# Turning two x1n tiles by VectorE and DRAM in place of TensorE in a retention and FFN kernel

## The chip, the cores and the metric

The kernel runs on one core of a Trainium2 chip. The metric is the device time of one execution in microseconds; the lower the better. A core has five engines that run their own instruction streams in order: TensorE (PE; its weight loads are a row of their own, PEld), VectorE (DVE), ScalarE (ACT), GpSimd (POOL) and SyncE (SP), which here issues nearly all DMAs.

## The reference

4096 tokens (4 sequences of 1024) of width 512 go through a retention layer and an FFN, each with a layer norm in front and behind:

```python
def attn(x):                       # x normalised
    q, v = x @ Wq.T, x @ Wv.T
    ret = scan(v)                  # state = lam * state + v_t, by head
    out = layernorm(q * ret) * gamma + beta
    return (out * silu(x @ Wg.T)) @ Wo.T

def ffn(x):                        # x normalised, weights rounded to fp8 and back
    gate = silu((x @ gate_w) * gate_scale)
    return ((gate * ((x @ up_w) * up_scale)) @ down_w) * down_scale

x1  = x  + layernorm(attn(layernorm(x)))
out = x1 + layernorm(ffn(layernorm(x1)))
```

Everything is float32. The inner width of the FFN is 1536.

## The kernel before

The tokens are cut into eight blocks of 512 (NB = 8), each of four tiles of 128 tokens. The main loop (lines 1048 to 1328) has one turn t for each block and in it twelve steps i, one for each 128 columns of the FFN's inner width. In step i of turn t TensorE does the gate, up and down matmuls of block t's FFN (`f`, an object of `Ffn`; down lags two steps behind), and between them pieces of the retention of block t + 1 (`b`) and, late in the turn, of block t + 2 (`n`). `l` is the FFN of the block before, whose end is done in the first steps. The order of all instructions on every engine is the order in which the code writes them (`InOrder`, line 66): a wait on an engine holds everything behind it on that engine.

**Retention of a block from 2 on ("fast").** Each of the four projections v, q, g, o is done as seven products on halves (a scheme after Strassen and Winograd), so a block has 28 products. `order` (line 333) is the list of them by projection and number j, and `product` (line 481) does the next one: 8 matmuls, then the work on the result (a copy, an addition into `mids`, for some j a scan or a gate), and it also issues the DMA that fetches the weights of the product four places on into a ring of four (`fetch_weights`, line 384). Right operands with sums in them are made on GpSimd by `input_sums` (line 465), which writes t_sums 0 to 3 from the turned input xnT: sums 1 and 2 serve products 5 and 6, sums 3 and 4 products 7 and 4. For v the order of j is 1, 2, 6, 7, 4, 5, 3. Product 2 of v ends in two scans on VectorE.

**From o to x1n.** When po of a tile is complete, `o_moments` takes its mean and variance on VectorE (bn_stats and bn_aggr) and the power -1/2 on GpSimd; `x1_of` normalises it on ScalarE (`shift_scale`), adds it to x on GpSimd and stores x1 to DRAM (`kept`); `x1_moments` does the statistics of x1; `x1n_of` normalises x1 on VectorE (`center_scale`). Then x1n has to be turned, so that the width lies along the partitions: the FFN's matmuls read it as x1nT, in two parts, an upper one (`upper_of`, a cast on ScalarE) and the rest (`rest_of`, a subtraction on VectorE).

In turns 1 to 5 the four tiles are turned in two ways. Tiles 0 and 1 go through `move_x1n` and `turn_by_blocks` (line 311): VectorE transposes blocks of 32 x 32, four DMAs a tile write them to DRAM with the blocks in their new places, one DMA loads the tile. Tiles 2 and 3 are turned by TensorE in step 11 (`turn_x1n`, line 751: four transposes a tile into PSUM, tile pt). The next turn's first gate (line 1088) reads all four tiles of x1nT, the whole of both parts.

The input of the block after, xn, is turned in the same turns by `send_x` and `fetch_x` (lines 443 and 457): VectorE transposes blocks, one DMA a tile writes them to DRAM (mx), and after the fourth tile four DMAs fetch a quarter of the partitions each into xnT.

**Order in steps 9 to 11 of turns 1 to 5**, by engine where it matters:

- Step 9: gate; the last product of o; x1_moments of tiles 0 and 1; up; fuse (VectorE multiplies gate and up, ScalarE casts the product); x1n_of, block transpose and DRAM writes of tiles 0 and 1, then their two loads; input_sums 1 and 2 of n; o_moments of tiles 2 and 3; down.
- Step 10: gate; x1_of of tiles 2 and 3; up; fuse; x1_moments of tiles 2 and 3; x1n_of of tile 2; down.
- Step 11: gate; up; n's product v1; fuse; x1n_of of tile 3; the rest of fuse of step 10 (`f.rest(10)`, in the other steps at the step's start); input_sums 3 and 4; upper and rest of tiles 0 and 1; down; transposes, upper and rest of tiles 2 and 3; n's products v2 and v6.
- Step 0 of the next turn: rest of fuse of step 11; gate; product v7; up; fuse; product v4; down; product v5.

In turn 6 there is no n; tiles 2 and 3 are turned by TensorE there too. In turn 1 ScalarE also runs a search for values out of range over the weights (`find_over`), whose scratch lies in buffers that the transposes use.

Of the kernel before, what the change touches and what calls it, by code (L numbers as in the profile page):

```python
# [10 lines left out]
F32 = mybir.dt.float32  # L11
# [6 lines left out]
P = 128  # L18
# [5 lines left out]
def retention_ffn_sandwich(  # L24
# [20 lines left out]
    NT, D = x.shape  # L45
    I = gate_w.shape[1]
    NC = D // P
# [3 lines left out]
    NB = NT // TB  # L51
    Q = 32
    NQ = P // Q
# [5 lines left out]
    work = ctx.enter_context(tc.tile_pool(name="work", bufs=2))  # L59
    small = ctx.enter_context(tc.tile_pool(name="small", bufs=3))  # L60
    dram = ctx.enter_context(tc.tile_pool(name="dram", bufs=2 * NS, space=bass.MemoryType.DRAM))
# [249 lines left out]
    def turn_by_blocks(dst, src, tag, name):  # L311


        t = work.tile([P, NQ, NC, Q], F32, tag=tag, name=name)
        dve.transpose(t, src.rearrange("p (c a i) -> p a c i", c=NC, a=NQ))
        m = dram.tile([P, NQ, NC, Q], F32, tag="turn", name=f"m{name}", bufs=3)
        for b in range(NQ):
            sp.dma_start(
                m[:, b].rearrange("(a i) c j -> i a (c j)", a=NQ),
                t[ts(b, Q)].rearrange("i a c j -> i a (c j)"),  # L320
            )
        return lambda: sp.dma_start(dst, m)
# [7 lines left out]

    FAST = 2
    H = TB // 2
    order = [("v", j) for j in (1, 2, 6, 7, 4, 5, 3)]
    order += [("q", j) for j in (1, 6, 2, 7, 4, 5, 3)]
    order += [("g", j) for j in (1, 2, 6, 7, 4, 5, 3)]
    order += [("o", j) for j in (1, 2, 6, 5, 3, 7, 4)]
    banks = {
        "v": {1: 0, 6: 1, 5: 0}, "q": {1: 1, 6: 0, 5: 1},
        "g": {1: 0, 6: 0, 5: 1}, "o": {1: 0, 6: 1, 5: 0},
# [38 lines left out]
            sp.dma_start(operands[k][j], t)  # L378

    RING = 4  # L380
    total_products = len(order) * (NB - FAST)
    fetched = [0]

    def fetch_weights():
        n = fetched[0]
        if n < total_products:
            k, j = order[n % len(order)]
            sp.dma_start(w_ring[:, n % RING], operands[k][j])
            fetched[0] += 1

    class Retention:
# [88 lines left out]

        def product(self):

            k, j = order[self.made]
            n = (self.t - FAST) * len(order) + self.made
            self.made += 1
            w = w_ring[:, n % RING]
            if j in (1, 6, 5):
                bank = ps_tile(f"p{k}{j}_{self.t}", f"pa{banks[k][j]}").rearrange("p (c f) -> p c f", c=2)
                if j == 6:
                    self.bank_b = bank  # L490
                else:
                    self.bank_a = bank
            bank = self.bank_b if j in (6, 7, 4) else self.bank_a
            for o in range(2):
                out_ = bank[:, o]
                if k != "o" and len(self.right[j].shape) == 4:
                    out_ = out_.rearrange("p (g j) -> p g j", j=Q)
                for c in range(2):
                    if k == "o":
                        left, right = self.left[j][:, c, ts(o, P)], w[:, c, :]  # L500
                    else:
                        left, right = w[:, c, ts(o, P)], self.right[j][:, c]
                    pe.matmul(
                        out_, left, right,
                        start=(j in (1, 6, 5) and o == 0 and c == 0), stop=True,
                        skip_group_check=True,
                    )
            fetch_weights()
            if k == "o":
                return self.add_o(j, bank)  # L510
            c12, p1, s167 = (mids[:, m] for m in (1, 2, 3))
            if k == "v" and self.t == FAST:

                if j == 1:
                    self.p1 = work.tile([P, 2, H], F32, tag="rstd", name="p1", bufs=1)
                p1 = self.p1
            if j == 1:
                act.copy(p1, bank)
            elif j == 6:
                dve.tensor_tensor(c12, bank, p1, ALU.add)  # L520
            elif j == 7:
                dve.tensor_tensor(s167, bank, p1, ALU.add)
            elif j == 2:
                self.take(k, 0, 0, bank)
            elif j == 4:
                dve.tensor_tensor(p1, bank, p1, ALU.add)
                self.take(k, 1, 0, p1)
            elif j == 5:
                dve.tensor_tensor(s167, bank, s167, ALU.add)
                self.take(k, 1, 1, s167)  # L530
            else:
                dve.tensor_tensor(c12, bank, c12, ALU.add)
                self.take(k, 0, 1, c12)
# [195 lines left out]
        def x1_of(self, s):  # L729
            self.x1n[s] = work.tile([P, D], F32, tag="tok", name=f"x1n_{self.t}_{s}", bufs=4)  # L730
            center = shift_scale if self.fast else self.center
            center(self.x1n[s], self.po.pop(s), self.mvo[s])
            pool.tensor_tensor(self.xt[s], self.xt[s], self.x1n[s], ALU.add)
            self.kept[s] = dram.tile([P, D], F32, tag="kept", name=f"kept_{self.t}_{s}")
            sp.dma_start(self.kept[s], self.xt[s])

# [17 lines left out]
        def move_x1n(self, s):  # L754

            x1n = self.x1n.pop(s)
            dst = x1n.rearrange("p (b c j) -> p b c j", b=NQ, c=NC)
            self.pt[s] = dst.rearrange("p b c j -> p c b j")
            return turn_by_blocks(dst, x1n, "ret", f"xs1_{self.t}_{s}")

        def part(self, h, s):
            part = self.x1nT[:, h, :, ts(s, P)]
# [152 lines left out]
    a = Retention(0, x_first)  # L915
# [84 lines left out]
    a.o_moments(0)  # L1000
    rounds(1)
    a.x1_of(0)
    a.o(1, "pd1")
    a.o_moments(1)
    a.x1_moments(0)
    a.x1_of(1)
    a.x1n_of(0)
    a.o(2, "pd2")
    a.o_moments(2)
    a.x1_moments(1)  # L1010
    a.x1_of(2)
    a.x1n_of(1)
    a.o(3, "pd3")
    a.new_x1nT()
# [2 lines left out]
    a.o_moments(3)  # L1017
    a.x1_moments(2)
    a.x1_of(3)
    a.x1n_of(2)  # L1020
    a.rest_of(0)
    b.q(0, "pf")
# [25 lines left out]
    for t in range(NB):  # L1048
        f, n = Ffn(a), None
        fast = b is not None and b.fast  # L1050
        for i in range(NI):
            if t > 0 and (t > 1 or i) and not (fast and i == 11):
                (f if i else l).rest((i - 1) % NI)
            if t == 0 and i == 0:
                n = Retention(2)
# [36 lines left out]
            for _ in range(look[i][0] if t == 1 else 0):  # L1092
                next(search)

            if fast and i < 10:
                b.product()
            if t == 2 and i == 0:
                next(passing)
# [44 lines left out]
            if fast and i == 7:  # L1143
                b.y_sums(3, 4)
            if fast and i == 9:
                b.x1_moments(0)
                b.x1_moments(1)
            if fast and i == 10:
                b.x1_of(2)
                b.x1_of(3)  # L1150
            units()
            f.up(i)
            if n and i == 11:
# [3 lines left out]
            if t == 0 and i == 10:  # L1157
# [1 line left out]
                keep_sums("g")  # L1159
                load()  # L1160
                b.o_moments(3)
            if b and i == 11:
                b.x1n_of(3, center_scale)
            if fast and i == 11:
                f.rest(10)
            if n and i == 11:
                n.input_sums(*((3, 4) if fast else (1, 2)))
            if t == 0 and i == 11:
                b.upper_of(2)
            if fast and i == 9:  # L1170
                loads = []
                for s in range(2):
                    b.x1n_of(s)
                    loads.append(b.move_x1n(s))
                for load in loads:
                    load()
                if n:
                    n.input_sums(1, 2)
            if fast and i == 11:
                for s in range(2):  # L1180
                    b.upper_of(s)
# [33 lines left out]
            if fast and i == 8:  # L1215
# [1 line left out]
                b.o_moments(1)  # L1217
                b.x1_of(0)
                b.x1_of(1)
            if fast and i == 9:  # L1220
                b.o_moments(2)
                b.o_moments(3)
            if fast and i == 10:
                b.x1_moments(2)
                b.x1_moments(3)
                b.x1n_of(2)
            if t == 0:
                if i == 3:
                    rounds(2, now=False)
                    b.halves()  # L1230
                    units()
                    rounds(1, now=False)
                elif i < 8:
                    rounds(3, now=False)
                if i == 2:
                    b.halves()
                if i < 11:
                    f.rest(i)
                if i < 2:
                    n.stats(i)  # L1240
# [7 lines left out]
                n.new_xnT()  # L1248
            if b and not fast and 7 <= i <= 10:
                b.x1_of(i - 7)  # L1250
            if b and not fast and i >= 9:
                b.rest_of(i - 9)
            if n and t > 0 and i in (6, 7):
# [28 lines left out]
            if n and i == 11:  # L1282
                if t == 0:
                    n.product()
                else:
                    b.turn_x1n(2, "pf")
                    b.upper_of(2)
                    b.rest_of(2)
                b.turn_x1n(3, "pf")
                b.upper_of(3)  # L1290
                b.rest_of(3)
                if t == 0:
                    n.input_sums(3, 4, engine=dve)
                    f.rest(11)
            if fast and (i < 3 or i in (7, 8)):
                b.product()
            if fast and i == 2:
# [6 lines left out]
                b.var()  # L1304
                b.rstd_y()
            if n and i == 11:
                n.products(2 if t else 1)
            if n and t > 0 and i == 5:
                n.stats(0)
                n.stats(1)  # L1310
# [86 lines left out]
```

## Time and profile before

| | us |
|---|---|
| median of 3 runs | 972.82 |
| lowest, highest | 972.75, 974.45 |
| the profiled execution | 973.82 |
| its span, first to last instruction | 972.0 |

The page of the profiled execution gives for each engine the time in which it was busy and the share of the span; "PE 957.4 (98%)" is TensorE's. The granted clock of TensorE was 0.997 of full speed. A line of the timeline gives start, duration, engine, code line, operation, tiles (out<-in) and shape, how many instructions it merges, and in brackets the idle time of the engine in front of it with what ended it. All code lines are L74, the helper that records every operation, so the tiles' names tell what a line is: pfg is the gate's result, pfu up's, pd down's, pv a product of v, pt the transposed x1n, t_sums the input sums, mx the DRAM copy of xn, mxs that of tiles 0 and 1 of x1n, mv the statistics.

The costliest groups of instructions by TensorE are up (205.1 us), gate (198.1) and down (189.4), 768, 768 and 720 matmuls of 128x512 that follow each other about 0.23 us apart. The 68 transposes into pt, 8 of them in each of turns 1 to 5, are recorded with 275 ns each; they overlap.

### The profile page before, as it was taken

The numbers are of one execution on the slowest core, as the hardware profiler recorded it, in microseconds if no ns is written. First come the engines' busy times: TensorE is split into PE (matmuls) and PEld (weight loads), VectorE is DVE, ScalarE is ACT, GpSimd is POOL, SyncE is SP. The second block draws the span as 40 slices with busy tenths as digits, with TensorE's granted clock in tenths as the row PEclk, the third lists the DMA queues.
The fourth block names the chain that finished last, engine by engine and source line by source line (L and its number), as shares of the span: only waits on it lengthen the run. The fifth ranks groups of instructions, "written<-read, shape, count | busy, mean of one in ns | idle before, by whom it ended". The sixth has DMA issues, their size and how long they took to land.

```text
span 972.0 us, 11798 instructions
## 1 busy us (share of the span) xinstructions
PE 957.4 (98%) x4118; PEld 764.9 (79%) x4118; DVE 678.5 (70%) x1038; ACT 406.2 (42%) x637; POOL 283.1 (29%) x356
## 2 busy tenths in 40 slices
PE   9999999999999999999999999999999999999996
PEld 7455767678888888888888888888888888888885
DVE  5996999666767577586685766867667676757535
ACT  3555675458655135431433315332153421524223
POOL 1405121402327042250523405242142512314020
PEclk9999999999999999999999999999999999999998
DMA  9311424753426326462236523364242632314021
GB/s 306 116 53 57 151 66 100 243 183 90 143 89 184 129 87 216 124 187 93 96 111 178 158 84 121 104 176 142 76 152 91 180 119 81 104 44 131 0 87 44
DMA packets 96060, 119.04 MB, mean 122 GB/s; under 512 B 8320, under 2 KB 58240, under 8 KB 96000
## 3 DMA queue, kind: packets, MB, share of 16 engines
q1 hardware_dynamic: 95136, 117.62, 39.4%
q8 instruction: 33, 0.54, 0.2%
q10 hardware_dynamic: 864, 0.66, 0.2%
q14 instruction: 27, 0.22, 0.1%
HBM read 86.00 MB, written 32.24 MB: 122 GB/s over the span
## 4 chain that ended last, share of the span: by engine, by line
PE 88%; DVE 6%; ACT 2%; POOL 2%; issue 1%; DMA 1%; SPq 0%; DVEq 0%; ACTq 0%; POOLq 0%
PE pfg L74 16%; PE pfu L74 16%; PE pd L74 15%; PE pq L74 10%; PE pv L74 10%; PE pg L74 9%; PE po L74 9%; DVE scr L74 1%; DVE st L74 1%; DVE y L74 1%; POOL mv L74 1%; PE pt L74 1%; PE idle L74 1%; ACT x1n L74 1%; POOL x L74 1%
## 5 line engine op out<-in xcount | busy, mean ns | idle before, releaser
L74 PE MATMUL pfu<-x1nT,up_sb 128*128 128x512 f32 x768 | 205.1, 409 | 0.0
L74 PE MATMUL pfg<-x1nT,gate_sb 128*128 128x512 f32 x768 | 198.1, 400 | 0.7 <-DVE x1nT L74 0.7
L74 PE MATMUL pd<-down_sb,fuse 128*128 128x512 f32 x720 | 189.4, 405 | 0.0
L74 PEld LDWEIGHTS pfu<-x1nT,up_sb 128*128 128x128 f32 x768 | 144.4, 188 | 32.2 <-issue 3.1
L74 PEld LDWEIGHTS pfg<-x1nT,gate_sb 128*128 128x128 f32 x768 | 144.1, 188 | 31.2 <-DVE x1nT L74 1.6
L74 PEld LDWEIGHTS pd<-down_sb,fuse 128*128 128x128 f32 x720 | 135.3, 188 | 27.5
L74 ACT ACTIVATE gate<-pfg,gs_sb 128x512 f32<-128x512 f32 x96 | 65.6, 683 | 169.5 <-PE pfg L74 169.3
L74 ACT CAST fuse<-gate 128x512 fp32r<-128x512 f32 x90 | 55.6, 618 | 176.0 <-DVE gate L74 175.8
L74 DVE SCALAR_TENSOR_TENSOR gate<-pfu,us_sb,gate 128x512 f32<-128x512 f32 x96 | 71.8, 747 | 57.3 <-PE pfu L74 55.9
L74 POOL TENSOR_SCALAR mv<-mv 128x1 f32<-128x1 f32 (+1 forms) x82 | 23.8, 290 | 263.9 <-DVE mv L74 260.7
L74 DVE TENSOR_TENSOR fuse<-gate,fuse 128x512 fp32r<-128x512 f32 x90 | 78.4, 871 | 5.5 <-ACT fuse L74 5.5
L74 POOL TENSOR_TENSOR ysum<-y 128x256 f32<-128x256 f32 (+1 forms) x14 | 14.3, 1023 | 198.6 <-DVE y L74 198.6
L74 DVE BATCH_NORM_STATS2 st<-x 128x6 f32<-128x512 f32 x64 | 43.6, 681 | 27.5 <-POOL x L74 24.8
L74 POOL TENSOR_TENSOR mv<-mv,nhalf 128x1 f32<-128x1 f32 (+1 forms) x75 | 48.6, 648 | 6.2
L74 PE MATMUL pv<-t_sums,w_ring 128*128 128x256 f32 x192 | 45.7, 381 | 1.1 <-DVE mids L74 0.5
L74 PE MATMUL po<-w_ring,t_sums 128*128 128x256 f32 x192 | 45.5, 379 | 0.3 <-issue 0.2
L74 POOL TENSOR_TENSOR x<-x,x1n 128x512 f32<-128x512 f32 x32 | 41.8, 1308 | 12.9 <-ACT x1n L74 12.4
L74 PE MATMUL pg<-t_sums,w_ring 128*128 128x256 f32 x192 | 45.5, 380 | 0.0
L74 PE MATMUL pq<-t_sums,w_ring 128*128 128x256 f32 x192 | 45.3, 379 | 0.0
L74 PEld LDWEIGHTS pv<-t_sums,w_ring 128*128 128x128 f32 x192 | 36.0, 189 | 7.7 <-DVE mids L74 0.9
L74 PEld LDWEIGHTS po<-w_ring,t_sums 128*128 128x128 f32 x192 | 36.2, 189 | 6.6 <-issue 1.1
L74 PEld LDWEIGHTS pg<-t_sums,w_ring 128*128 128x128 f32 x192 | 35.9, 189 | 6.4 <-ACT mids L74 1.2
(168 smaller groups left out, 1512.3 us busy)
## 6 DMA issues: line engine op xcount, KB each, us to landing
kept<-x SPq DMA_DIRECT2D x32, 256.0 KB, 3.1
x<-kept SPq DMA_DIRECT2D x32, 256.0 KB, 3.9
x<-in_x SPq DMA_DIRECT2D x28, 256.0 KB, 4.3
out<-d SPq DMA_DIRECT2D x27, 256.0 KB, 2.1
xnT<-mx SPq DMA_DIRECT2D x24, 256.0 KB, 5.0
w_ring<-dsum_v SPq DMA_DIRECT2D x24, 256.0 KB, 3.6
w_ring<-dsum_q SPq DMA_DIRECT2D x24, 256.0 KB, 2.6
w_ring<-dsum_g SPq DMA_DIRECT2D x24, 256.0 KB, 2.7
```

What stands on the lines that cost most here:

```text
L74: return lambda *args, **kwargs: tc.keep_in_program_order(op(*args, **kwargs))
```

## The change

- `order` is written out for all blocks from 2 on, and v's order of j is 1, 6, 2, 7, 4, 5, 3 for the blocks after block 2.
- The store of x1 is taken out of `x1_of` into `keep_x1`, and the calls are placed one by one.
- In turns 1 to 6 the statistics of po of tiles 2 and 3 move in front of the statistics of x1 of tiles 0 and 1: o_moments(2), (3) to step 9 before up; x1_moments(0), (1) and x1_of(2), (3) behind fuse in step 9. x1n_of(3) moves from step 11 to step 10, and `f.rest(10)` to the start of step 11.
- In turns 1 to 5 tiles 2 and 3 are no longer turned by TensorE. `send_pair` in step 10 transposes blocks on VectorE and writes each tile with one DMA to DRAM; `fetch_pair` in step 11 loads both tiles with four DMAs, a quarter of the partitions each. upper and rest of these tiles read the loaded pair.
- input_sums 1 and 2 move to the end of step 10, behind `send_pair`.
- In turns 1 to 5 step 11 does four products of v: v1 after up as before, v6 and v2 after down, v7 behind upper and rest of tiles 2 and 3. Step 0 of turns 2 to 6 does one product less.

```diff
-    order = [("v", j) for j in (1, 2, 6, 7, 4, 5, 3)]
-    order += [("q", j) for j in (1, 6, 2, 7, 4, 5, 3)]
...
+    for t in range(FAST, NB):
+        order += [("v", j) for j in ((1, 2, 6, 7, 4, 5, 3) if t == FAST else (1, 6, 2, 7, 4, 5, 3))]
...
+        def keep_x1(self, s):
             self.kept[s] = dram.tile([P, D], F32, tag="kept", name=f"kept_{self.t}_{s}")
             sp.dma_start(self.kept[s], self.xt[s])
...
+        def send_pair(self):
+
+            self.m = dram.tile([2 * P, D], F32, tag="turn_pair", name=f"mp_{self.t}", bufs=2)
+            for s in (2, 3):
+                sq = work.tile([P, D], F32, tag="ret", name=f"xs1_{self.t}_{s}")
+                dve.transpose(
+                    sq.rearrange("p (a c j) -> p a c j", a=NQ, c=NC),
+                    self.x1n.pop(s).rearrange("p (c a i) -> p a c i", c=NC, a=NQ),
+                )
+                sp.dma_start(self.m[ts(s - 2, P), :], sq)
+
+        def fetch_pair(self):
+            pair = work.tile([P, 2, NQ, NC, Q], F32, tag="xn", name=f"pair_{self.t}", bufs=1)
+            for a in range(NQ):
+                sp.dma_start(
+                    pair[ts(a, Q)].rearrange("p k g c j -> p (k g) (c j)"),
+                    self.m[:, ts(a, P)].rearrange("(g i) f -> i g f", i=Q),
+                )
+            for s in (2, 3):
+                self.pt[s] = pair[:, s - 2].rearrange("p g c j -> p c g j")
...
-            if t > 0 and (t > 1 or i) and not (fast and i == 11):
+            if t > 0 and (t > 1 or i):
                 (f if i else l).rest((i - 1) % NI)
...
-            if fast and i < 10:
+            if fast and i < 10 and (i or b.t == FAST):
                 b.product()
...
             if fast and i == 9:
-                b.x1_moments(0)
-                b.x1_moments(1)
-            if fast and i == 10:
-                b.x1_of(2)
-                b.x1_of(3)
+                b.o_moments(2)
+                b.o_moments(3)
             units()
             f.up(i)
...
-            if b and i == 11:
+            if t == 0 and i == 11:
                 b.x1n_of(3, center_scale)
-            if fast and i == 11:
-                f.rest(10)
...
             if fast and i == 9:
+                b.x1_moments(0)
+                b.x1_moments(1)
+                b.x1_of(2)
+                b.x1_of(3)
                 loads = []
                 for s in range(2):
                     b.x1n_of(s)
                     loads.append(b.move_x1n(s))
+                b.keep_x1(2)
+                b.keep_x1(3)
                 for load in loads:
                     load()
-                if n:
-                    n.input_sums(1, 2)
+            if n and fast and i == 11:
+                b.fetch_pair()
...
             if fast and i == 10:
                 b.x1_moments(2)
                 b.x1_moments(3)
                 b.x1n_of(2)
+                b.x1n_of(3)
+                if n:
+                    b.send_pair()
+                    n.input_sums(1, 2)
...
                 else:
-                    b.turn_x1n(2, "pf")
-                    b.upper_of(2)
-                    b.rest_of(2)
-                b.turn_x1n(3, "pf")
-                b.upper_of(3)
-                b.rest_of(3)
+                    n.products(2)
+                    for s in (2, 3):
+                        b.upper_of(s)
+                        b.rest_of(s)
...
             if n and i == 11:
-                n.products(2 if t else 1)
+                n.product()
```

More of the change, by code (lines that the diff above doesn't have):

```diff
@@ L332, in retention_ffn_sandwich @@
     H = TB // 2
-    order = [("v", j) for j in (1, 2, 6, 7, 4, 5, 3)]
-    order += [("q", j) for j in (1, 6, 2, 7, 4, 5, 3)]
-    order += [("g", j) for j in (1, 2, 6, 7, 4, 5, 3)]
-    order += [("o", j) for j in (1, 2, 6, 5, 3, 7, 4)]
+    order = []
+    for t in range(FAST, NB):
+        order += [("v", j) for j in ((1, 2, 6, 7, 4, 5, 3) if t == FAST else (1, 6, 2, 7, 4, 5, 3))]
+        order += [("q", j) for j in (1, 6, 2, 7, 4, 5, 3)]
+        order += [("g", j) for j in (1, 2, 6, 7, 4, 5, 3)]
+        order += [("o", j) for j in (1, 2, 6, 5, 3, 7, 4)]
     banks = {
@@ L380, in retention_ffn_sandwich @@
     RING = 4
-    total_products = len(order) * (NB - FAST)
+    total_products = len(order)
     fetched = [0]
@@ L386, in fetch_weights @@
         if n < total_products:
-            k, j = order[n % len(order)]
+            k, j = order[n]
             sp.dma_start(w_ring[:, n % RING], operands[k][j])
@@ L481, in product @@
         def product(self):
-            k, j = order[self.made]
-            n = (self.t - FAST) * len(order) + self.made
+            n = (self.t - FAST) * (len(order) // (NB - FAST)) + self.made
+            k, j = order[n]
             self.made += 1
@@ L1002, in retention_ffn_sandwich @@
     a.x1_of(0)
+    a.keep_x1(0)
     a.o(1, "pd1")
@@ L1006, in retention_ffn_sandwich @@
     a.x1_of(1)
+    a.keep_x1(1)
     a.x1n_of(0)
@@ L1011, in retention_ffn_sandwich @@
     a.x1_of(2)
+    a.keep_x1(2)
     a.x1n_of(1)
@@ L1019, in retention_ffn_sandwich @@
     a.x1_of(3)
+    a.keep_x1(3)
     a.x1n_of(2)
@@ L1219, in retention_ffn_sandwich @@
                 b.x1_of(1)
-            if fast and i == 9:
-                b.o_moments(2)
-                b.o_moments(3)
+                b.keep_x1(0)
+                b.keep_x1(1)
             if fast and i == 10:
@@ L1250, in retention_ffn_sandwich @@
                 b.x1_of(i - 7)
+                b.keep_x1(i - 7)
             if b and not fast and i >= 9:
@@ L1284, in retention_ffn_sandwich @@
                     n.product()
-                else:
-                    b.turn_x1n(2, "pf")
-                    b.upper_of(2)
-                    b.rest_of(2)
-                b.turn_x1n(3, "pf")
-                b.upper_of(3)
-                b.rest_of(3)
-                if t == 0:
+                    b.turn_x1n(3, "pf")
+                    b.upper_of(3)
+                    b.rest_of(3)
                     n.input_sums(3, 4, engine=dve)
                     f.rest(11)
+                else:
+                    n.products(2)
+                    for s in (2, 3):
+                        b.upper_of(s)
+                        b.rest_of(s)
             if fast and (i < 3 or i in (7, 8)):
```

## The prediction

> **What bounds the kernel now.** I read the page's busy shares first, then the waits, then the timeline around the place of the change. TensorE is busy for nearly the whole span:
>
> ```profile
> PE 957.4 (98%) x4118; PEld 764.9 (79%) x4118; DVE 678.5 (70%) x1038; ACT 406.2 (42%) x637; POOL 283.1 (29%) x356
> PE   9999999999999999999999999999999999999996
> ```
>
> No other engine is near. In the list of who waited for whom, TensorE's waits come to some 6 us, most of it in the first 200 us. Of the tiles that the change touches it names x1nT once (at the end of block 0) and x1n once (in block 5):
>
> ```profile
> PE pfg L74 <- DVE x1nT L74: 0.7, 1, 0.7
> PE pt L74 <- DVE x1n L74: 0.5, 1, 0.5
> ```
>
> So matmul work that goes is a gain, and every microsecond that TensorE is made to wait is a loss; work on the other engines is free until it makes TensorE wait. Step 11 of FFN block 2, TensorE alone (start, duration, operation):
>
> ```profile
> 427.04 2.18 PE L74 MATMUL pd<-down_sb,fuse 128*128 128x512 f32 x8
> 429.06 1.03 PE L74 MATMUL pt<-ident,x1n 128*128 128x128 f32 x8
> 429.93 1.89 PE L74 MATMUL pv<-xnT,w_ring 128*128 128x256 f32 x8
> 431.66 1.89 PE L74 MATMUL pv<-t_sums,w_ring 128*128 128x256 f32 x8
> 433.20 2.19 PE L74 MATMUL pfg<-x1nT,gate_sb 128*128 128x512 f32 x8
> 435.23 1.89 PE L74 MATMUL pv<-t_sums,w_ring 128*128 128x256 f32 x8
> ```
>
> From start to start: the eight transposes of tiles 2 and 3 (pt) take 0.87 us, a product 1.73, a product in front of a gate 1.54. The gate of the next block, at 433.20, reads all four tiles of x1nT, so it is where a late tile stops TensorE.
>
> [...]A sum of GpSimd starts at 427.05 and takes 1.29; VectorE's x1n beside it takes 1.50 where the same form just before took 0.55, and the SBUF+SBUF subtraction that follows takes 1.78 beside the next sum (its form alone: 0.68):
>
> ```profile
> 425.86 0.55 DVE L74 TENSOR_SCALAR x1n<-x,mv 128x512 f32<-128x512 f32 x1
> 427.12 1.50 DVE L74 TENSOR_SCALAR x1n<-x,mv 128x512 f32<-128x512 f32 x1
> 428.54 1.78 DVE L74 TENSOR_TENSOR fuse<-gate,fuse 128x512 fp32r<-128x512 f32 x1
> ```
>
> A block transpose in such company (at 418.45, beside a sum of 418.21 to 419.57) still took 0.71. [...]The trace's own rows for the twin of the new transfer, xn through DRAM (mx) into xnT,[...] give its price: 256 KB out in about 2.1 us, and back in pieces of 512 bytes, here the first and the last of four, each asked for alone:
>
> ```profile
> mx<-xn SPq DMA_DIRECT2D x1, 256.0 KB, 2.3
> xnT<-mx SPq DMA_DIRECT2D x1, 256.0 KB, 3.2
> xnT<-mx SPq DMA_DIRECT2D x1, 256.0 KB, 5.9
> ```
>
> **What goes.** In blocks 1 to 5 the eight transposes: 5 x 0.87 = 4.4 us of TensorE. In block 5 the second tile's transposes waited for x1n (0.46 in the timeline), and from the transposes' start to the gate it takes 4.83 us there against 4.14 in block 2, so 0.69 more goes. Ceiling of the gain: 5.0 us. The product that moves from step 0 into step 11 costs TensorE the same in both places (435.23 - 433.20 + 1.53 to the next start, less the 1.81 of a gate followed by an up, is 1.75); it only puts the gate later by 1.73, which is time lent to the transfer. ScalarE's and VectorE's copies of tiles 2 and 3 (upper, rest) stay, from SBUF in place of PSUM.
>
> **What comes, step by step, in block 2.** All starts from VectorE's last addition to po, at 412.99, which the change doesn't move.
>
> VectorE now takes o_moments(2), (3) at 413.60 in place of x1_moments(0), (1): same operations, so fuse(9) stays at 415.28 to 416.03. Then x1_moments(0), (1), 1.75, to 417.7. x1n(0) waits for GpSimd's power (0.82 behind the statistics), 417.75 to 418.3, transpose to 419.0. x1n(1) meets GpSimd's addition x1(2), which now lies at about 418.6 to 419.9 (ScalarE's shift-scale starts behind its cast of 416.07): to 420.2, transpose to 420.9. rest(9), two SBUF inputs, waits out the addition x1(3): to 421.9. fuse(10): to 422.6. x1_moments(2), (3): to 424.25. x1n(2): to 424.85. x1n(3) waits for its power at 425.15 and then runs beside the first of the moved GpSimd sums, as today's at 427.12 does: 1.50, to 426.7. Two transposes, 0.71 each, overlapping a little: to 428.05. This is the row of steps I trust least: without the collision it ends 1.0 earlier, with one more 0.6 later.
>
> SyncE has by then issued the eight writes of tiles 0 and 1 (as today, some 2 us later), two stores of x1, two loads and the first half of the pair; all wait for things done by 424.3, so nothing holds the second half. It is written at 428.1 and lands 2.1 later (2.0 to 2.4 in rows without a queue in front), 430.2. The weights of the first product, once issued at 427.42, now stand behind that write and land some 1.3 later; they are used in the next step 0, so this costs nothing.
>
> fetch_pair needs both halves in DRAM. Its four transfers are of 128 KB, which no row shows. In the twin, 256 KB take 1.36 us each behind a base of 1.85 (3.2 for the first, 7.3 from the first issue to the last landing); half of that is 0.68 each, 1.85 + 4 x 0.68 = 4.57. Bounds: the issues alone, 0.48 apart, would end at 3.95; with other traffic or a cost by transfer, 5.5. I take 4.57: landed at 434.8.
>
> Then ScalarE's two casts (1.07 in today's rows) and VectorE's second subtraction. In block 6, where all this is visible without company, the gate starts 1.90 behind the first cast (894.33 to 896.23). So the gate could start at 436.7. VectorE has the two scans of product 2 in front of these subtractions; product 2 ends near 432.6 and the scans take 1.3 (today's rows), 434.0, so they are hidden by the transfer. Without that cover they would hold the gate to some 435.4.
>
> TensorE itself would be ready at 429.06 + 1.73 + 1.73 + 1.54 = 434.06. So it waits 2.6 us. Against that stand 0.87 saved: +1.75 a block, five blocks 8.75, less block 5's 0.69: **+8.1 us**.
>
> **Edits at nothing.** Sums 1 and 2 for product 6: done near 428.2, needed at 429.06; 0.9 to spare, and a delay would only eat into the wait behind it. Sums 3, 4: done by 431.5, needed at 432.5 and later. rest(10) earlier, x1(0), x1(1) stored a little later: used far off. In block 1 ScalarE's search for overflow needs the buffer that the first half leaves (near 429.6 in block 2's times), which delays its copy of product 1 and product 2 by about 1 us; the gate's wait shrinks by as much. Block 6 keeps its transposes and gains 0.2 at most. Block 0 and the tail don't change.
>
> The profiled execution took 973.82 (span 972.0, so 1.8 lie outside), the median is 972.82; the difference goes on the median: **980.9 us**.
>
> **Rivals.** *A, all hidden (faster).* If the chain on VectorE and the transfer together are 2.6 us shorter than I reckon, the gate meets no wait: 972.8 - 5.0 = 967.8. For it: 1.75 us of cover were put in by the product, and today's collision might fall differently. Against it: VectorE has hardly a gap between 413 and 428, and my shortest figures (1.0 + 0.6 + 0.1) save 1.7, not 2.6. *B, gain and wait cancel.* With just those shortest figures the wait is 0.9, as much as the transposes: 972.8 + 5 x 0.05 - 0.7, near 972.4. *C, longer waits.* The longest figures (0.6, 0.9, 0.3) add 1.8 a block: 990.[...] *D, the change doesn't do what it says*: no, pt leaves blocks 1 to 5 by construction; only block 0, one tile of block 1's and block 6 keep it.
>
> **How the numbers follow.** Forecast case (waits of 1.7 to 4 us) 0.64; A 0.13; B 0.10; C 0.13. The range of 972.5 to 988 takes in B, the forecast and half of C, and leaves out A. What this kernel's measurement can tell from no change is about 0.2%, 1.9 us: faster is A, same is B, slower the forecast and C.
>
> **What would show it.** Right: no pt in step 11 of blocks 1 to 5; pfg waiting there for x1nT, some 2.6 us, five times; the last transpose of the pair 15.1 us behind the last addition to po; landing 6.7 behind that. Wrong: gates without a wait (A), a wait in front of a product for t_sums or mids in place of the gate's, or matmuls slower than 0.23 apart behind the gap (C).

## The result and the profile after

| | before | after |
|---|---|---|
| median (lowest to highest), us | 973.17 (972.75 to 974.45, 4 runs) | 988.71 (987.48 to 990.83, 4 runs) |
| ratio, 95% interval | | 1.0157 [1.0144, 1.0170] |
| the profiled execution, its span | 973.82, 972.0 | 989.39, 987.6 |
| granted clock in it | 0.997 | 0.996 |

It is slower by 15.5 us, about twice the 8.1 forecast, and 0.7 above the top of the stated range (988). Page of the kernel after, busy time by engine:

```profile
PE 958.4 (97%) x4078; PEld 761.2 (77%) x4078; DVE 685.1 (69%) x1048; ACT 406.1 (41%) x637; POOL 283.0 (29%) x356
```

There are 40 matmul records fewer (the transposes), and yet PE is busy 1 us longer, the first hint that some matmuls ran slower. The waits of TensorE in the kernel after (who waited for whom, total us, times, longest):

```profile
PE pfg L74 <- ACT x1nT L74: 5.8, 5, 1.6
PE pv L74 <- issue: 5.1, 5, 1.0
PE pfg L74 <- DVE x1nT L74: 3.2, 7, 1.2
PE pv L74 <- ACT mids L74: 1.7, 1, 1.7
```

The forecast was a wait at the gate in each of five turns. Of the five waits for ScalarE four are in turns 2 to 5 (1.1 to 1.6); the fifth (0.6) is behind turn 6, which has no pair. In turn 1 the gate waits only for VectorE's rest, 0.2. The second line was not in the forecast: a product, five times 1.0. Step 11 of block 2, TensorE in the timeline of the kernel after:

```profile
432.06 1.89 PE L74 MATMUL pv<-t_sums,w_ring 128*128 128x256 f32 x8
433.79 1.89 PE L74 MATMUL pv<-xnT,w_ring 128*128 128x256 f32 x8
436.70 1.97 PE L74 MATMUL pv<-t_sums,w_ring 128*128 128x256 f32 x8 [1.03 <-issue]
439.92 0.50 PE L74 MATMUL pfg<-x1nT,gate_sb 128*128 128x512 f32 x1 [1.25 <-ACT x1nT L74]
440.73 1.88 PE L74 MATMUL pfg<-x1nT,gate_sb 128*128 128x512 f32 x7 [0.31 <-DVE x1nT L74]
```

Three stops: v7 (1.03), the gate's first matmul for ScalarE's cast (1.25), its second for VectorE's rest (0.31). VectorE before that, same step and kernel, from the last addition to po at 415.97:

```profile
415.97 0.69 DVE L74 TENSOR_TENSOR mids<-po,mids 128x512 f32<-128x512 f32 x1 [2.26 <-PE po L74]
...
419.90 0.66 DVE L74 BATCH_NORM_STATS2 st<-x 128x6 f32<-128x512 f32 x1
421.25 0.18 DVE L74 BATCH_NORM_AGGREGATE mv<-st 128x2 f32<-128x6 f32 x1 [0.69 <-ACT x1n L74]
...
422.58 1.50 DVE L74 TENSOR_SCALAR x1n<-x,mv 128x512 f32<-128x512 f32 x1
...
429.21 1.48 DVE L74 TENSOR_SCALAR x1n<-x,mv 128x512 f32<-128x512 f32 x1 [0.44 <-POOL mv L74]
430.61 1.29 DVE L74 STREAM_TRANSPOSE xs<-x1n 128x512 f32<-128x512 f32 x2
...
434.34 1.66 DVE L74 TENSOR_TENSOR x1nT<-x1n,x1nT 128x512 fp32r<-128x512 f32 x2 [1.20 <-ACT x1nT L74]
435.92 0.68 DVE L74 TENSOR_TENSOR mids<-pv,mids 128x512 f32<-128x512 f32 x1
```

The pair's transposes end at 431.90, 15.93 behind the addition (forecast 15.06). Nearly all of the difference is one idle stretch, 0.69: a small aggregate that stands still "<-ACT x1n". It writes an mv tile; mv has three buffers, and the new order asks for four before the first has been read out, by ScalarE's normalisation of po's tile 2 (x1n here). The two last lines show what v7 waited for: v6's addition into mids stands on VectorE behind the rests of tiles 0 and 1, and ends at 436.60; v7 starts at 436.70.

The DMAs of the kernel after in this stretch (number, size of one, median us to landing):

```profile
mp<-xs SPq DMA_DIRECT2D x2, 256.0 KB, 2.1
pair<-mp SPq DMA_DIRECT2D x4, 128.0 KB, 2.8
```

The second half's write lands 2.27 behind its issue; the four loads follow the last landing at once, and the last of them lands 4.36 behind the first issue, at 438.63. ScalarE's cast starts at 438.73.

**Where the 15.6 us lie.** I compared the start of the second matmul of each block's first gate (the first one that has all its data) in both traces, and took out 1.75 for the product that now stands in front of it:

| stretch (to the next block's first gate) | forecast | after − before |
|---|---|---|
| up to block 1's gate | 0 | 0.72 |
| turn 1 | 1.75 | 2.78 |
| turn 2 | 1.75 | 1.86 |
| turn 3 | 1.75 | 1.99 |
| turn 4 | 1.75 | 4.95 |
| turn 5 | 1.06 | 1.77 |
| turn 6 (no pair) | 0 | 1.34 |
| tail | 0 | 0.16 |
| sum | 8.06 | 15.57 |

Step by step inside the turns, at the gate itself turn 3 loses 2.5 and not 2.0 (4.13 at the gate, less 1.63 that step 0 no longer spends on v7). A stall of 0.4 in step 8 comes and goes (as the timelines read, a product's place in PSUM, the memory that the matmuls write, waits for VectorE behind the transpose of xn): before has it in blocks 2 and 3, after only in block 4. It gives 0.4 back in turns 2 and 3 and takes 0.5 in turn 4.

Turn 4 stands out because of the clock. Busy time by stretch at block 4's first gate, kernel after; "PEclk" is the granted clock:

```profile
core 0: us, PE busy (x) PEld busy (x) DVE busy (x) ACT busy (x) POOL busy (x), PEclk, DMA share, GB/s
550.00:559.60 9.60, 7.02 (x31) 5.23 (x30) 6.91 (x12) 2.79 (x5) 3.54 (x3) 1.00 0.76 221
559.70:563.10 3.40, 3.40 (x9) 2.62 (x9) 0.87 (x2) 0.47 (x1) 0.00 (x0) 0.50 0.86 311
563.20:575.00 11.80, 11.80 (x55) 9.99 (x54) 7.07 (x12) 1.43 (x3) 0.00 (x0) 1.00 0.18 52
```

Right behind the stops, nine matmuls in 3.4 us, 0.43 apart in place of 0.23, at a clock of 0.50. By estimate that costs half of the 3.41 us, 1.7.

### The profile page after: what moved, and what is told of

Read it like the earlier page. It is cut to its first block, busy times and chain, and to the rows that moved or that the text cites. A ratio compares the mean times of both kernels' runs of the same rounds, so it can differ in the third digit from the quotient of the medians.

```text
span 987.6 us, 11758 instructions
## 1 busy us (share of the span) xinstructions
PE 958.4 (97%) x4078; PEld 761.2 (77%) x4078; DVE 685.1 (69%) x1048; ACT 406.1 (41%) x637; POOL 283.0 (29%) x356
## 4 chain that ended last, share of the span: by engine, by line
PE 74%; DVE 13%; ACT 4%; issue 3%; DMA 3%; POOL 2%; SPq 1%; DVEq 0%; ACTq 0%; POOLq 0%
PE pfg L74 14%; PE pfu L74 13%; PE pd L74 12%; PE pq L74 10%; PE pg L74 9%; PE po L74 8%; PE pv L74 6%; DVE st L74 2%; DVE gate L74 2%; DVE fuse L74 2%; DMA pair<-mp 1%; DVE xs L74 1%; DVE x1n L74 1%; POOL mv L74 1%; ACT x1n L74 1%
## 5 line engine op out<-in xcount | busy, mean ns | idle before, releaser
L74 PE MATMUL pfg<-x1nT,gate_sb 128*128 128x512 f32 x768 | 200.7, 402 | 9.0 <-ACT x1nT L74 5.8
L74 DVE TENSOR_TENSOR fuse<-gate,fuse 128x512 fp32r<-128x512 f32 x90 | 73.4, 815 | 5.5 <-ACT fuse L74 5.5
```

Source lines behind the costliest of these rows:

```text
L74: return lambda *args, **kwargs: tc.keep_in_program_order(op(*args, **kwargs))
```

## The experiments

Theory: the loss is the transfer of the pair, which holds the gate, made longer by the mv ring and by stretches at half clock. Rivals: v7's wait is the loss; GpSimd's moved sums hold VectorE; the new order costs by itself. Each ratio is against runs of the kernel before on the same chip (medians 973.63, 973.20 and 972.92); a difference to the changed kernel's 988.71 is across chips, and good to some 0.7.

### e1: mv with a fourth buffer

```diff
-        mv = small.tile([P, 2], F32, tag="mv", name="mv")
+        mv = small.tile([P, 2], F32, tag="mv", name="mv", bufs=4)
-        st = small.tile([P, 6], F32, tag="st", name="st")
+        st = small.tile([P, 6], F32, tag="st", name="st", bufs=2)
```

(st gives the room.)

> The changed kernel with four buffers for the statistics mv instead of three (and two in place of three for bn_stats' output, to make room). Theory 1 (the gate of the next block waits for one chain: statistics and x1n on VectorE, the pair's way through DRAM, the last casts): the second statistics of x1 no longer wait 0.7 us for ScalarE to have read the first mv, the chain is 0.7 shorter in each of turns 1 to 6, and the time falls by 4 us to about 984.6. Rival (what counts is product v7, which waits 1.0 us behind v6's addition): no change, 988.7. Rival (what counts is the clock at half after the gaps): unchanged to within the spread, 987 to 991.

Measured: 982.39 (981.62 to 984.99), ratio 1.0097 [1.0084, 1.0110], 6.3 below the changed kernel. The timeline of e1 at the same place:

```profile
418.66 0.66 DVE L74 BATCH_NORM_STATS2 st<-x 128x6 f32<-128x512 f32 x1
419.35 0.18 DVE L74 BATCH_NORM_AGGREGATE mv<-st 128x2 f32<-128x6 f32 x1
```

The stop is gone, and the chain from the addition to the last transpose is 15.16. Turns 1, 2, 3 and 5 lose 0.7 to 0.8 less each (1.99, 1.19, 1.20, 0.96), turn 6 0.9 less (0.48). That is some 4.7 if turn 4 is counted alike; most of the rest can be put down to the clock, for this trace has no stretch at half clock in mid-kernel (mean granted clock 0.998; the gate waits 0.52 in place of 1.25). That the ring is a cost is shown.

### e2: v7 back in step 0

```diff
-            if fast and i < 10 and (i or b.t == FAST):
+            if fast and i < 10:
                 b.product()
...
-            if n and i == 11:
+            if n and i == 11 and t == 0:
                 n.product()
```

> The changed kernel with product v7 back in step 0 of the next turn. Theory 1: the gate starts when it did, since it waits for the pair and not for v7, and the 1.75 us of v7 come on top in each of five turns: 997.5. [...]Rival (v7's wait for v6's addition is on the path): the wait of 1.0 goes, 983.5.

Measured: 1007.82 (1003.29 to 1009.59), ratio 1.0347 [1.0327, 1.0366]. More than the product's 1.7 a turn. The timeline and the stretches of e2:

```profile
443.78 4.16 PE L74 MATMUL pfg<-x1nT,gate_sb 128*128 128x512 f32 x8 [5.79 <-ACT x1nT L74]
```

```profile
core 0: us, PE busy (x) PEld busy (x) DVE busy (x) ACT busy (x) POOL busy (x), PEclk, DMA share, GB/s
430.00:441.20 11.20, 7.98 (x37) 6.50 (x35) 8.23 (x13) 2.25 (x4) 6.89 (x7) 1.00 0.64 207
441.40:448.10 6.70, 4.31 (x9) 3.10 (x10) 1.90 (x3) 1.26 (x3) 0.00 (x0) 0.50 0.66 234
448.30:455.00 6.70, 6.70 (x31) 5.65 (x31) 2.99 (x5) 0.98 (x2) 0.00 (x0) 1.00 0.17 55
```

The gate's 8 matmuls take 4.16 where the kernel before takes 2.19: from each of these gaps on (4.2 to 5.8, turns 2 to 5) the clock is at a half for 6.8 us, and in turn 1, where the gate waits 2.48 and 0.48, for 3.4 (mean granted clock of this execution: 0.983). So v7 in front of the gate is cover that works, and in this trace the half clock comes with the gaps.

### e6: e2 with the gap filled

e2, and in front of the first gate of blocks 2 to 6:

```diff
+            if i == 0 and 2 <= self.t <= 6:
+                for _ in range(18):
+                    pe.matmul(pg, mean_r, down_sb[:, 0, :], start=True, stop=True)
             project(pg, gate_sb, i, self.parts)
```

> The kernel with v7 back in step 0 (1007.8), and 18 matmuls of 128x512 of no use in front of the first gate of blocks 2 to 6, 4.1 us, to fill TensorE's wait (their result is overwritten). Clock theory[...]: the trace shows no half clock there any more and the time falls by 10 us to 995 to 998, which is the changed kernel plus 5 x 1.75. Rival (the 10 us come from another wait): 1007 or more.

Measured: 1001.12 (1000.03 to 1001.74), ratio 1.0289 [1.0275, 1.0303], above the expected range, but 6.7 below e2 though TensorE does 90 matmuls more. The same stretch of e6, columns as above:

```profile
441.40:448.10 6.70, 4.70 (x20) 3.45 (x19) 1.90 (x3) 1.83 (x3) 0.00 (x0) 1.00 0.66 232
```

There are 20 matmuls where e2 has 9, at full clock, and no stretch at half clock is left in the kernel's middle (mean granted clock 0.998, e2's 0.983). The added matmuls change nothing but TensorE's activity, and can only delay a gate, so the clock is worth at least the 6.7: this is shown.

### e3: sums 1 and 2 back at the end of step 9

```diff
                     b.send_pair()
-                    n.input_sums(1, 2)
...
                 for load in loads:
                     load()
+                if n:
+                    n.input_sums(1, 2)
```

> The changed kernel with GpSimd's input sums 1 and 2 back in step 9. Theory 1: x1n of tile 3 no longer meets a GpSimd sum (1.48 us instead of 0.55), so the chain is 0.6 to 0.9 shorter in five turns: 984.2 to 985.7. Rival: the sums then hold GpSimd's powers behind them, or meet the subtraction of step 9, and nothing is won: 988.7 or up to 990.

Measured: 994.40 (992.23 to 996.54), ratio 1.0215 [1.0199, 1.0232]. The theory missed: slower, by 5.7 over the changed kernel. GpSimd and VectorE in e3's timeline:

```profile
428.33 1.30 POOL L74 TENSOR_TENSOR t_sums<-xnT,t_sums 128x512 f32<-128x512 f32 x1
429.72 0.19 POOL L74 TENSOR_SCALAR mv<-mv 128x1 f32<-128x1 f32 x1
...
430.58 0.55 DVE L74 TENSOR_SCALAR x1n<-x,mv 128x512 f32<-128x512 f32 x1 [1.20 <-POOL mv L74]
431.57 1.50 DVE L74 TENSOR_SCALAR x1n<-x,mv 128x512 f32<-128x512 f32 x1 [0.45 <-POOL mv L74]
```

The statistics of tile 2 were there at 428.58, but the power that turns them into a scale stands behind two sums on GpSimd's queue. And the collision is not avoided: x1n of tile 3 takes 1.50 beside sum 3 in place of sum 1. The chain is 17.01 long. The move of the sums, which I had put at no cost, is what keeps the powers early; it is one of the parts that help.

### e4: no way through DRAM

```diff
-                sp.dma_start(self.m[ts(s - 2, P), :], sq)
+                self.pt[s] = sq.rearrange("p (a c j) -> p c a j", a=NQ, c=NC)
...
-                b.fetch_pair()
```

(and the search's scratch of turn 1 in other buffers). The exchange of blocks is left out, so the gate reads tiles 2 and 3 not fully turned.

> The changed kernel without the pair's way through DRAM: upper and rest of tiles 2 and 3 read the block-transposed tile itself, so these tiles are not fully turned (left out: the exchange of blocks; one scratch buffer of the search in turn 1 is another one). Theory 1: 6.6 us of the chain go, but VectorE's two scans of product v2 then stand in front of the last subtractions, so the gate comes only 1.6 earlier in each of five turns: 980.5. Rival (transfer is the whole of the wait): all waits go, 968 to 970. Rival (v7 is what counts): little change, 986 to 989.

Measured: 980.92 (978.93 to 982.87), ratio 1.0077 [1.0065, 1.0089], as expected. The way through DRAM, with what hangs on it (the search's buffer, the clock), is worth 7.8, half of the loss. Its timeline:

```profile
434.99 1.97 PE L74 MATMUL pv<-t_sums,w_ring 128*128 128x256 f32 x8 [1.07 <-issue]
436.60 2.60 PE L74 MATMUL pfg<-x1nT,gate_sb 128*128 128x512 f32 x8
```

Without the transfer the gate follows at once, and v7's wait is what remains in front of it in turns 1 to 5, with 0.1 to 0.2 for VectorE's rest. So the transfer is not the whole story: with it gone the kernel still doesn't gain. Of the 6.7 by which this trace is longer than before's, turns 1 to 5 have 3.5, turn 6 has 2.3 (0.85 of it a wait of ScalarE for the load of an earlier tile), and 0.9 lies in front of block 1's gate.

### e5: the new order alone, tiles 2 and 3 turned by TensorE

```diff
                 else:
-                    n.products(2)
                     for s in (2, 3):
+                        b.turn_x1n(s, "pf")
                         b.upper_of(s)
                         b.rest_of(s)
+                    n.product()
...
-                    b.send_pair()
                     n.input_sums(1, 2)
...
-                b.fetch_pair()
```

(and step 0 keeps its product, as before.)

> The changed kernel with tiles 2 and 3 turned by TensorE again and product v7 back in step 0: what stays of the change is the moved statistics, normalisations and input sums, and the order of v's products. Theory 1: the moved order alone makes fuse(11) on VectorE and with it the casts of all four tiles late, as in turn 6 of the changed kernel; each gate waits 0.7 to 1.3 us in six turns: 977 to 981. Rival (the order is free, the DRAM way is the whole loss): 972 to 974.

Measured: 977.49 (976.12 to 978.07), ratio 1.0045 [1.0033, 1.0058]. The order costs 4.3 with nothing sent through DRAM. In its trace 1.2 of that is turn 6, and turns 1 to 4 lose 0.7 each up to the gate, of which step 8's stall gives some back; turn 5 loses nothing, for before waited there itself. The waits of e5, then one line of VectorE and one of TensorE in its block 2:

```profile
PE pt L74 <- DVE gate L74: 2.2, 5, 0.4
```

```profile
419.24 0.18 DVE L74 BATCH_NORM_AGGREGATE mv<-st 128x2 f32<-128x6 f32 x1 [0.69 <-ACT x1n L74]
...
431.08 0.66 PE L74 MATMUL pt<-ident,x1n 128*128 128x128 f32 x4 [0.45 <-DVE gate L74]
```

VectorE is late with the multiplication of step 11, and with it the PSUM tile that the second transpose needs. The statistics put in front and x1n(3) moved up may be the cause; but e5 keeps the three mv buffers, and the ring's stop of 0.69 is in it too, longer than the 0.45 that the transpose waits. No run has this order with four buffers, so how much of the 4.3 is the ring's and how much the order's own stays open.

### e7: e1, with v6's addition in front of the rests of tiles 0 and 1

```diff
-                    b.rest_of(s)
+                    if not n:
+                        b.rest_of(s)
...
-                    n.products(2)
+                    n.product()
+                    b.rest_of(0)
+                    b.rest_of(1)
+                    n.product()
```

> The kernel with four mv buffers (982.4) and v6's addition in front of the rest subtractions of tiles 0 and 1 on VectorE in turns 1 to 5, so that v7 doesn't wait for it. Theory 1: v7's wait of 1.07 goes, and the gate waits as much longer, since it waits for the pair: 981.5 to 982.5 (a few tenths in turn 1, where v7 is last). Rival (v7's wait is part of the loss): 977.

Measured: 989.42 (983.85 to 991.58), ratio 1.0160 [1.0133, 1.0187]: a miss of 7, slower than e1. Its timeline, and the stretch behind it in e7 and then in e1 (columns as in e2):

```profile
438.19 4.16 PE L74 MATMUL pfg<-x1nT,gate_sb 128*128 128x512 f32 x8 [2.99 <-ACT x1nT L74]
```

```profile
437.50:444.30 6.80, 6.09 (x14) 4.43 (x15) 2.49 (x4) 1.33 (x3) 0.00 (x0) 0.50 0.49 162
```

```profile
437.50:444.30 6.80, 5.97 (x26) 4.78 (x26) 3.24 (x5) 1.83 (x4) 0.00 (x0) 1.00 0.61 195
```

v7's wait is gone, and the gate comes no earlier for the transfer (only in turn 1, by 0.5), so TensorE's idle time now lies in one piece. The line shows the longest of them: in this turn the fetch took 5.64 where e1's takes 4.46. In turns 3 to 5 the gate waits 1.75 to 1.83. From these waits on the clock falls in four turns (14 matmuls at 0.50 in e7's line, 26 at 1.00 in e1's): for 3.4 us in three turns and 6.8 in one, 17 us in all at half speed (mean granted clock 0.989), which by estimate lose up to half of that, 8.5. That refutes the rival that v7's wait is the loss: it lay inside the gate's.

### e8: one tile by VectorE and DRAM

From the kernel before: tile 2 alone goes through DRAM, tile 3 stays with TensorE and stands behind v6, the statistics keep their old order, v's order and v7 in step 11 as in the change.

```diff
+                if n:
+                    b.send_one(2)
...
-                else:
-                    b.turn_x1n(2, "pf")
-                    b.upper_of(2)
-                    b.rest_of(2)
+                n.product()
                 b.turn_x1n(3, "pf")
                 b.upper_of(3)
                 b.rest_of(3)
+                if t:
+                    b.upper_of(2)
+                    b.rest_of(2)
```

(send_one and its fetch are send_pair and fetch_pair for one tile.)

> The kernel before with tile 2 alone turned by VectorE and DRAM in turns 1 to 5, in the old order of the statistics, v's new order of products and v7 in step 11 (v6 in front of tile 3's transposes). Theory 1: tile 2 is normalised 1.3 us before tile 3 and its way is shorter (one write, half the bytes back), so its casts are done by 434.1 in block 2's times, when TensorE gets to the gate at 434.5; four transposes a turn are saved, 5 x 0.43: 970.7. Rival (any way through DRAM from step 10 is too late): waits of 1 us and more, 975 to 980.

Measured: 970.89 (969.96 to 972.44, 17 runs) against 973.20, ratio 0.9980 [0.9973, 0.9987]: faster than both. TensorE in its timeline:

```profile
430.27 0.60 PE L74 MATMUL pt<-ident,x1n 128*128 128x128 f32 x4
430.71 1.89 PE L74 MATMUL pv<-xnT,w_ring 128*128 128x256 f32 x8
432.44 1.89 PE L74 MATMUL pv<-t_sums,w_ring 128*128 128x256 f32 x8
433.98 2.20 PE L74 MATMUL pfg<-x1nT,gate_sb 128*128 128x512 f32 x8
```

There is no stop at all. Half of the transposes gone in five turns is 5 x 0.44 = 2.2, and 2.3 came. VectorE's one transpose of this kind ends at 426.16, where the pair's end at 431.90 in the changed kernel, and half of the bytes take the way through DRAM. e8 differs from the change in two things, the one tile and the old order of the statistics (which has no stop of the ring); they were not tested apart.

### e9: turn 1's search in other buffers

```diff
-                    tag = "ret" if k >= 18 else "xn"
+                    tag = "ret" if 18 <= k < 23 else "xn"
```

(and the same in the buffer count.)

> The changed kernel, but the search over the weights in turn 1 keeps its scratch out of the buffers that the pair's transposes use. Its copy of product v1 then no longer waits, so product v2 starts some 1.7 us earlier, the gate of block 2 behind it 0.7 to 0.9 earlier; turn 1 costs 1.9 in place of 2.8. Theory: 987.9 (0.7 to 0.9 below the 988.7 of the changed kernel). Rival of the prediction (the gate waits for the pair anyway and takes in the delay): 988.7, no change.

Measured: 988.01 (987.20 to 989.44), ratio 1.0157 [1.0143, 1.0171]. The medians alone can't tell this from no change. In the trace v2's wait of 1.7 for ScalarE's copy is gone, and turn 1 loses 0.46 less (2.32 in place of 2.78): between the two expectations. v2's delay was partly taken in by the gate's wait, as forecast, and partly not.

### e10: the gate's gap filled in the changed kernel

As e6's edit, with `range(6)` and v7 left in step 11.

> The changed kernel, with six matmuls whose result is thrown away in front of the first gate of blocks 2 to 6, where TensorE waits some 1.3 us for the pair; six of them take about 1.4 us. The answer is computed as before. Theory (some of these gaps put the clock to half for 3.4 us, which costs 1.7 each, once or twice in an execution): no stretch at half clock is left, 985.5 to 987, and the single times lie closer together than the 3.3 us of the changed kernel. Rival (what turn 4 loses beyond the others isn't the gap's): the six matmuls can only add, 988.7 to 989.5.

Measured: 987.78 (987.31 to 990.71), ratio 1.0159 [1.0145, 1.0173]: between the two expectations, and one run as slow as ever, so as a timing it is inconclusive. Its trace says more:

```profile
439.00 1.75 PE L74 MATMUL pfg<-down_sb,mean_r 128*128 128x512 f32 x6
440.59 0.49 PE L74 MATMUL pfg<-x1nT,gate_sb 128*128 128x512 f32 x1
```

No stretch at half clock is left in mid-kernel (mean granted clock 0.997); turn 4 loses 2.33 in place of 4.95. But in turn 1, where the gate hardly waits for the pair, the six matmuls add 1.0. The two together are 1.7 of the 1.9 by which its span is shorter. The run of 990.71 had a mean clock of 0.997, so it isn't explained by the clock; that stays open.

## Why the prediction was right, and where it was wrong

**Right: the direction and its cause.** The gate of the next block waits for the pair in turns 1 to 5; in turn 1 only for 0.2, since v2 and v7 have waited 2.8 in front of it. The 0.87 a turn that the transposes no longer take is less than these waits. Taking the way through DRAM out (e4) gives back 7.8.

**Right: the transfer.** The write was put at 2.1 and took 2.27; the fetch at 4.57, from half of the twin's 1.36 a transfer, and took 4.36 (4.3 to 4.4 in all five turns). From the first cast to the gate 1.90 was used; the gate's second matmul comes 2.00 behind it. TensorE alone would have been ready at 434.06; v2's start and the two products' time give 433.79 + 1.73 + 1.54 − 2.98 (by which the addition to po came later than before) = 434.08. The fetch was a term worked out from rows of its twin, and it held.

**Wrong: "to 428.05", VectorE's chain.** It was 0.87 longer, 0.69 of it the fourth mv in a ring of three. The step "VectorE now takes o_moments(2), (3) at 413.60 in place of x1_moments(0), (1): same operations" looked at the operations and not at which buffers are still held: the reader of the first mv on ScalarE now comes behind three more writers. From start to start the gate's second matmul stood 3.4 behind what TensorE could do, where 2.6 was forecast for the gate. e1 shows the price: 0.7 to 0.8 a turn. The collisions with GpSimd were forecast at the right places; x1n of tiles 1 and 3 took 1.50 and 1.48, those of tiles 0 and 2, with no 128x512 operation of GpSimd beside them, 0.51 and 0.55.

**Wrong: the clock (rival C).** I put slower matmuls at the far end of the longest waits, at 2.6 + 1.8 = 4.4; that was an estimate, which no trace had shown. In the profiled run it came behind stops of 1.25 and 0.31 close together (and one of 1.02 some 2 us ahead of them), and cost 1.7 there, in one turn of five. e2, e6 and e7 tie it to the gaps: 0.50 behind e2's 5.79 and e7's 2.99, 1.00 where e6 fills e2's gap. Over all the timed runs its share can't be read exactly; their mean clocks are 0.994 to 0.996 against 0.997 before, of 988 us some 1 to 3.

**Wrong: "Block 6 … gains 0.2 at most".** Turn 6 lost 1.34. It takes the new order too, with its mv stop (e1: 0.48 is left without it), and VectorE is late for the last multiplication and the rests. The kernel before and the kernel after, VectorE in turn 6, from the last addition to po to the multiplication of step 11:

```profile
879.20 0.69 DVE L74 TENSOR_TENSOR mids<-po,mids 128x512 f32<-128x512 f32 x1 [1.46 <-PE po L74]
...
891.98 0.75 DVE L74 SCALAR_TENSOR_TENSOR gate<-pfu,us_sb,gate 128x512 f32<-128x512 f32 x1
```

```profile
893.05 0.69 DVE L74 TENSOR_TENSOR mids<-po,mids 128x512 f32<-128x512 f32 x1 [1.45 <-PE po L74]
...
907.40 0.74 DVE L74 SCALAR_TENSOR_TENSOR gate<-pfu,us_sb,gate 128x512 f32<-128x512 f32 x1
```

12.78 became 14.35. "Edits at nothing" had the transposes in view, not the order around them; e5 loses 1.2 in turn 6, with the same stop of the ring in it.

**Half right: the search in turn 1.** The delay of product 2 was put at "about 1 us" and was 1.74; "the gate's wait shrinks by as much" held for most of it, but 0.46 reached the gate (e9).

**Not seen, and without price: v7 behind v6's addition.** The prediction let TensorE reach the gate without a stop. v7 stopped for 1.0 a turn, inside the time in which the gate would have waited anyway, and e7 shows that its removal gains nothing; with the piece of work in the middle of the gap the clock even stayed at 1.00 (e1), without it it was 0.50 (e7). But e4 shows what it is when the gate doesn't wait: with the transfer gone it is the stop that remains.

**The sum.** Against the forecast the ring's stop makes turns 1 to 5 longer by 0.7 to 0.8 each (3.8, by e1), turn 6 adds 1.3, one stretch at half clock 1.7 and turn 1's search 0.5, and step 8's stall takes off 0.3. With 0.9 in the first stretch and the tail this is 7.9; the two traces have 7.5 between forecast and profile, so the account closes to 0.4. The 0.72 before any changed work came out between −0.7 and +1.0 in the other runs and is not the change's.

**Rivals A and B** needed a shorter chain than reckoned. e1 has about the forecast's chain (15.16) and loses 1.5 to 1.8 at the gates of turns 2 to 4, beside the 1.75 of the forecast: with the ring's stop taken out, the working holds.

## What to carry to other kernels

When instructions are put in a new order, count for each small ring of buffers how many are asked for before the first is read; an operation of 0.18 us can hold a whole engine (here VectorE, for 0.69). Work taken from the bounding engine is a gain only if what replaces it comes in time: e8 sends one tile of two the slow way, the one that is ready earlier, leaves the late one and the order where they were, and gains. A stop of the matmul engine can cost more than its length: e7, with the stop in one piece, had some 17 us at half clock and took 7.0 us more than e1, where v7 splits it; e2, with gaps of 4.2 to 5.8, took 6.7 more than e6, where they are filled. So it paid here to split a stop by useful work, or to fill it.

## What the hardware showed that I had not expected

Half clock came behind stops far shorter than 4.4 as well, and of like stops only some were followed by it. In the kernel after the stops around block 4's first gate (1.02, 1.25, 0.31) had 3.41 us at 0.50 behind them, from 559.67; the 3.41 us in front of that hold 1.56 of TensorE's idle time. The stops of block 2 (1.03, 1.25, 0.31) had none: the clock stayed at 1.00. Nor had 1.74 of idle time in the 3.41 us from 313.91, in turn 1. In e7 waits of 1.75 to 1.83 were followed in turns 3 to 5, while in e6 1.69 and 0.32, behind the added matmuls, were not (1.00 from 441.40 to 448.10). So in these traces the length of the stops alone doesn't tell which of them cost anything more; what does wasn't shown. Nor is it shown whether this is why the changed kernel's runs lie 3.3 us apart: the slowest has the lowest mean clock (0.994), but the fastest has 0.995 and the two between them 0.996.

GpSimd's queue is the other: in e3 a power of 0.55 us that waited behind two sums put a VectorE operation 1.2 us late, more than the collision that the move was meant to avoid.
